# Expert weights in pairs and by layer: a new order of loading in a Mixture-of-Experts stage on one Trainium2 core

## Chip, cores and metric

One core of one Trainium2 chip. The metric is the device time of one execution in microseconds (us); given is the median of the runs. The program is written in a tile language: a pool hands out buffers, and the framework puts in the waits between engines.

## What is computed

The input x has shape (4, 128, 64, 64). Layer 0 is group normalisation, three 1x1 convolutions and a full softmax attention over 4096 positions. Layer 1 treats the positions as tokens of 128 channels: first a cumulative attention with eight heads, then a feed-forward block in which each of 64 experts chooses 8 tokens of each batch entry. Only this last block matters here:

```python
pooled = jnp.einsum('bked,bke->bed', gathered, topv)       # 4 x 64 x 128
h = jnp.concatenate([pooled.transpose(1, 0, 2), ones], axis=-1)
h = jax.nn.gelu(jnp.einsum('ebd,edh->ebh', h, weight1), approximate=False)
h = jnp.concatenate([h, ones], axis=-1)
out = jnp.einsum('ebh,eho->ebo', h, weight2)               # 64 experts, 128 -> 512 -> 128
outputs = outputs.at[jnp.arange(Bn)[:, None], flat_idx].add(weighted)
```

Each expert sees one pooled row for each of the 4 batch entries, so its two matrices (128 x 512 and 512 x 128, 256 KB each in float32) are used for 4 rows only. The 64 experts have 32 MB of weights together, and all of them are read.

## The kernel before

The layers run one after the other; the expert block comes last, its first matmul at 2313.5 us of 2414.9. Its weights lie in DRAM as `fw`, one row block for each expert: 128 partitions x (512 numbers of the first layer + 512 of the second), 512 KB in one transfer. They are kept in NW = 21 buffers: 19 from the pool `fw`, and the two resident tensors `wks` and `wvs`, which held projections of the attention before (L1135 to L1140). The 21 first loads are given out ahead of the block (L1142). All of these loads stand on SP's queue, in the order in which the source gives them out, apart from `wks` and `wvs`, whose loads stand first. A load waits on SP for the buffer's last reader, and for the eighth load before it.

The experts go in 16 groups of QG = 4. The four experts of a group lie in four strips of 32 rows of one PSUM tile, so that their matmuls run side by side. The order of PE is written out by hand (`manual_schedule`, L1176). The steps for a group g are:

- `first(g)` (L1248): four matmuls 4 x 512 into `ph`; ScalarE copies them to `hr`.
- `turn(g)` (L1261): four transposes of `hr` (`htr`), VectorE adds the bias (`hs`), ScalarE applies GELU.
- `second(g)` (L1276): sixteen matmuls into `po`, the chunk c outside, the expert u inside; VectorE copies `po` to `og`. At its end, L1287 gives out the loads of the four experts that take over the group's buffers.
- `gather(g)` (L1291): a transpose of `og` and a copy into `eot`.
- `back(n)` (L1157), as filler between: turns four blocks of the residual `t` back into channel order (`otr`) and copies them.

In the loop (L1305), groups 0 to 4 (g < AHEAD = 5) run turn(g), first(g+1), back, gather(g-1), second(g); from group 5 on it is back, turn(g), back, gather(g-1), second(g), first(g+1). Three groups before the end the fillers stop. Also in the loop, ScalarE counts chosen tokens (L1320).

After the last group the result is transposed (L1334), and for the two pairs p of batch entries 16 tiles each are made by matmul (`sct`, L1357), added to `t` by VectorE (L1364) and written out from SP's and ScalarE's queues (L1367). At the very end a test value `inside` is made (L1373, L1374); every engine loads it into a register (L1380) and branches on it (L1381). With these inputs the branch's fallback is not taken.

Of the kernel before, what the change touches and what calls it, by code (L numbers as in the profile page):

```python
# [18 lines left out]
def conv_attn_hybrid_kernel(  # L19
# [55 lines left out]
    all_ones = const.tile([P, P], F32, tag="all_ones", name="all_ones")  # L75
# [26 lines left out]
    wks = resid.tile([C, NH, C], F32, tag="wks", name="wks")  # L102
    wvs = resid.tile([C, HD], F32, tag="wvs", name="wvs")
# [210 lines left out]
    with ExitStack() as l0:  # L314
# [261 lines left out]
        first, chain, blocks = preparation(0)  # L576
# [9 lines left out]
        for n, (b, qb, p) in enumerate(steps):  # L586
# [11 lines left out]
            if (qb, p) == (q0, 0) and b + 1 < B:  # L598
                first, chain, blocks = preparation(b + 1)
# [43 lines left out]
    inside = resid.tile([P, 1], mybir.dt.int32, tag="inside", name="inside")  # L643
    within = resid.tile([P, 1], F32, tag="within", name="within")
# [19 lines left out]
    QG = 4  # L664
    QW = P // QG
# [4 lines left out]
    EG = E // QG  # L670
    NB = B * NBLK
    NW = 21

    def layer1(pre, ready):
# [6 lines left out]
        with ExitStack() as kept, ExitStack() as l1:  # L681
# [447 lines left out]
            expert_weights = {}  # L1129

            def load_expert(e):
                if e >= E:
                    return

                if e % NW >= NW - 2:  # L1135
                    w = wvs if e % NW == NW - 1 else wks.rearrange("d h e -> d (h e)")
                else:
                    w = fwp.tile([P, FH + FC * C], F32, tag="fw", name=f"{pre}fw_{e}")
                nc.sync.dma_start(out=w, in_=fw[e])
                expert_weights[e] = (w[:, :FH], w[:, FH:].rearrange("p (c o) -> p c o", c=FC))  # L1140

            for e in range(NW):  # L1142
                load_expert(e)

            eos = fo.tile([P, B // 2, C], F32, tag="eo", name=f"{pre}eo")

# [6 lines left out]
            pooled = fo.tile([C, E, B], F32, tag="pooled", name=f"{pre}pooled")  # L1153
# [18 lines left out]
            def backs(m, engine):  # L1172
                for _ in range(m):
                    back(turns.pop(0), engine)

            with tc.manual_schedule(engines={mybir.EngineType.PE}):  # L1176
# [71 lines left out]
                def first(g):  # L1248

                    ph = phs[g % 2]  # L1250
                    for u in range(QG):
                        e = g * QG + u
                        nc.tensor.matmul(
                            ph[u * QW : u * QW + B, :], pooled[:, e, :], expert_weights[e][0],
                            start=True, stop=True,
                        )
                    hr = fs.tile([P, FH], F32, tag="hr", name=f"{pre}hr_{g}")
                    nc.scalar.copy(hr, ph)
                    return hr

                def turn(g, hr):  # L1261

                    ptr = ps_a.tile([P, FC, QG, QW], F32, tag="kv", name=f"{pre}htr_{g}")
                    for c in range(FC):
                        nc.tensor.transpose(
                            ptr[:, c].rearrange("p u b -> p (u b)"), hr[:, bass.ts(c, P)], ident
                        )
                    hs = fs.tile([P, FC, QG, B], F32, tag="hs", name=f"{pre}hs_{g}")
                    nc.vector.tensor_tensor(
                        hs, ptr[:, :, :, :B],  # L1270
                        fb1s[:, bass.ts(g, QG), :].rearrange("p u c -> p c u")
                        .unsqueeze(3).to_broadcast([P, FC, QG, B]), ALU.add,
                    )
                    return hs, nc.scalar.activation(hs, hs, AF.Gelu).ins

                def second(g, hs):  # L1276
                    po = pos[:, g % 2, :]
                    for c in range(FC):
                        for u in range(QG):
                            nc.tensor.matmul(  # L1280
                                po[u * QW : u * QW + B, :], hs[:, c, u, :],
                                expert_weights[g * QG + u][1][:, c, :],
                                start=(c == 0), stop=(c == FC - 1),
                            )
                    og = fs.tile([P, C], F32, tag="og", name=f"{pre}og_{g}")
                    nc.vector.tensor_copy(og, po)
                    for u in range(QG):  # L1287
                        load_expert(g * QG + u + NW)
                    return og

                def gather(g, og):  # L1291
# [10 lines left out]
                hr = first(0)  # L1302
                og = None
                AHEAD = NW // QG
                for g in range(EG):  # L1305
                    last = g + 3 >= EG
                    if turns and g >= AHEAD and not last:
                        backs(1, nc.vector)
                    hs, gelu = turn(g, hr)
                    if g < AHEAD:  # L1310
                        hr = first(g + 1)
                    if turns and not last:
                        backs(1, nc.vector)
                    if og is not None:
                        gather(g - 1, og)
                    if ready:
                        p, k = g // NBLK, g % NBLK
                        ones_of = ps_a.tile([P, BLK], F32, tag="kv", name=f"{pre}chosen_{g}")
                        with tc.issue_after(gelu):
                            nc.scalar.activation(  # L1320
                                ones_of, lgs[p][:, bass.ts(k, BLK)], AF.Sign,
                                accum_out=count[:, p, k : k + 1],
                            )
                    og = second(g, hs)
                    if AHEAD <= g < EG - 1:
                        hr = first(g + 1)
                    if turns and g in (AHEAD, AHEAD + 1):
                        with tc.issue_after(gelu):
                            backs(1, nc.scalar)
                assert not turns  # L1330
                gather(EG - 1, og)
                for p in range(B // 2):
# [3 lines left out]
                        out=eos[:, p, :], in0=ptr, scalar=rden[:, p : p + 1], in1=eos[:, p, :],  # L1336
                        op0=ALU.mult, op1=ALU.add,
                    )
                if ready:
                    chosen = fs.tile([P, 4], F32, tag="chosen", name=f"{pre}chosen", bufs=1)  # L1340
# [3 lines left out]
                        out=chosen[:, 3:4], in0=chosen[:, 2:3], scalar1=8.5, scalar2=None, op0=ALU.is_le  # L1344
                    )

                for p in range(B // 2):

                    for k0, OB in ((0, 1), (1, 1), (2, 2), (4, 2), (6, 1), (7, 1)):
                        for k in range(k0, k0 + OB):  # L1350
                            pss = [
                                ps_a.tile([P, BLK], F32, tag="kv", name=f"{pre}sct_{p}_{k}_{z}")
                                for z in range(2)
                            ]
                            for z in range(2):
                                half = slice(z * E, (z + 1) * E)
                                nc.tensor.matmul(  # L1357
                                    pss[z], eos[half, p, :], lgs[p][half, bass.ts(k, BLK)],
                                    start=True, stop=True,
                                )  # L1360
                            for z in range(2):
                                n = (2 * p + z) * NBLK + k
                                at = t[:, bass.ts(n, CPB), :].rearrange("c i x -> c (i x)")
                                nc.vector.tensor_add(at, at, pss[z])  # L1364
# [13 lines left out]

    layer1("", True)
    inside_r = nc.values_load(inside[0:1, 0:1], min_val=0, max_val=1)  # L1380
# [59 lines left out]
```

## Time and profile before

| | us |
|---|---|
| median of 3 runs | 2416.25 (2414.59 to 2419.01) |
| the profiled execution | 2416.65 |
| its span in the trace | 2414.9 |
| matmuls of the expert block, from the first to the last | 2313.5 to 2382.0 |
| first and last load of `fw` issued | 2278.8 and 2368.0 |
| output additions (L1364), 32 | 2385.3 to 2404.5 |

The engines: PE is TensorE's matmuls and PEld its weight loads, DVE is VectorE, ACT ScalarE, POOL GpSimd, SP SyncE, which issues most of the DMAs; "SPq" is its queue. Times in the trace are counted from the start of the span. Of the whole span PE is busy for 97%, nearly all of it in the two attentions; the mean DMA rate over the span is 46 GB/s, while in the last two of 40 equal slices it is 358 and 286 GB/s. PE's clock was granted at 0.994 of full speed on average. Each matmul of the source shows as two in the trace. A matmul's end in the trace is modelled, and a few matmul records can be missing.

### The profile page before, as it was taken

The page shows a single profiled execution, that of the slowest core. Times are in us where ns is not written, and L with a number is a line of the kernel's source. Part 1 is how long each engine was busy: PE and PEld are TensorE (multiplying, and loading weights), DVE is VectorE, ACT ScalarE, POOL GpSimd, SP SyncE. Part 2 cuts the span into 40 slices and gives each one's busy share as a digit, 9 for nine tenths or more (in the row PEclk, how much of TensorE's full clock was granted, in tenths as well). Part 3 has the DMA queues.
Part 4 walks back from the last instruction along what each step waited for, and adds up shares of the span by engine and source line. Part 5 has one row for each costly group of instructions (what it writes and reads, how often), then busy time and mean ns, then how long its engine had stood idle before and what let it go on. Part 6 is the DMA issues. An engine that isn't in the chain of part 4 may idle for free.

```text
span 2414.9 us, 45766 instructions
## 1 busy us (share of the span) xinstructions
PE 2347.5 (97%) x19496; PEld 1566.0 (65%) x19496; DVE 1505.8 (62%) x2610; ACT 1208.4 (50%) x1638; POOL 304.1 (13%) x337
## 2 busy tenths in 40 slices
PE   6999999999999999999999998999999999999887
PEld 3567777677778677778777774555555555555553
DVE  5666666666655666655555555666666676776654
ACT  4444444444443444444433434666666666666541
POOL 0000000000000000000000001334333433333200
PEclk9999999999999999999999999999999999999999
DMA  2200120000100000020000000211112121112397
GB/s 76 80 22 7 29 62 1 12 18 22 49 24 1 16 13 22 18 51 1 1 1 1 1 1 19 53 39 44 48 38 54 37 55 37 38 38 54 93 358 286
DMA packets 61191, 109.95 MB, mean 46 GB/s; under 512 B 10033, under 2 KB 35121, under 8 KB 60977
## 3 DMA queue, kind: packets, MB, share of 16 engines
q1 hardware_dynamic: 57536, 101.22, 14.5%
q10 hardware_dynamic: 3440, 5.70, 0.7%
q8 instruction: 155, 2.54, 0.4%
q14 instruction: 60, 0.48, 0.1%
HBM read 85.40 MB, written 8.91 MB: 39 GB/s over the span
## 4 chain that ended last, share of the span: by engine, by line
PE 89%; DVE 5%; ACT 2%; DMA 2%; issue 1%; SPq 0%; ACTq 0%; DVEq 0%
PE av L513 36%; PE sc L488 18%; PE pk L731 9%; PE pv L849 8%; PE po L885 4%; PE pt L865 2%; PE ps L750 2%; DMA fw<-in_fw_dram 1%; PE otr L552 1%; PE po L892 1%; PE pe L430 1%; PE pa L455 1%; PE pl L942 1%; DVE t L1364 1%; PE ltr L721 1%
## 5 line engine op out<-in xcount | busy, mean ns | idle before, releaser
L513 PE MATMUL av<-pr,am 64*128 64x512 f32 x4096 | 1050.5, 591 | 0.7 <-ACT pr L492 0.7
L495 DVE TENSOR_TENSOR acc<-acc,pr 128x1024 f32<-128x1024 f32 x480 | 586.8, 1223 | 443.4 <-ACT pr L492 443.2
L492 ACT ACTIVATE pr<-sc 128x1024 f32<-128x1024 f32 x512 | 523.6, 1023 | 671.8 <-PE sc L488 603.0
L513 PEld LDWEIGHTS av<-pr,am 64*128 64x128 f32 x4096 | 636.6, 187 | 253.2 <-issue 32.3
L488 PE MATMUL sc<-e,e 64*128 64x512 f32 x2048 | 608.0, 592 | 0.0
L488 PEld LDWEIGHTS sc<-e,e 64*128 64x128 f32 x2048 | 315.2, 187 | 103.1 <-issue 14.5
L731 PE MATMUL pk<-xt,wks 128*128 128x512 f32 x512 | 244.2, 617 | 6.7 <-DVE within L660 4.2
L849 PE MATMUL pv<-wvs,xt 128*128 128x512 f32 x512 | 226.4, 595 | 2.2 <-ACT v L853 2.2
L853 ACT ACTIVATE v<-pv 128x512 f32<-128x512 f32 x256 | 152.7, 597 | 69.7 <-PE pv L849 69.6
L733 ACT ACTIVATE ks<-pk 128x512 f32<-128x512 f32 x256 | 148.5, 597 | 62.8 <-PE pk L731 62.6
L849 PEld LDWEIGHTS pv<-wvs,xt 128*128 128x128 f32 x512 | 96.9, 191 | 121.0 <-issue 113.9
L837 DVE TENSOR_TENSOR em<-em,rb 128x1024 f32<-128x1024 f32 x64 | 79.5, 1244 | 148.0 <-DMA rb<-rd 148.0
L731 PEld LDWEIGHTS pk<-xt,wks 128*128 128x128 f32 x512 | 92.1, 193 | 115.0 <-issue 82.1
L828 POOL TENSOR_TENSOR em<-et,mask 128x1024 f32<-128x1024 f32 x64 | 122.6, 1937 | 88.3 <-ACT et L815 88.3
L96 POOL TENSOR_SCALAR xg<-t,gmv,grs 128x128 f32<-128x128 f32 x120 | 95.2, 806 | 285.9 <-DVE grs L92 207.4
L885 PEld LDWEIGHTS po<-v,em 64*64 64x64 f32 x4096 | 111.6, 133 | 27.3 <-DVE before L875 26.7
L885 PE MATMUL po<-v,em 64*64 64x128 f32 x4096 | 119.6, 271 | 0.3 <-issue 0.3
L739 POOL MEMSET ew<- 128x1024 f32 x1 | 1.0, 952 | 942.1 <-PE pa L455 942.1
L787 DVE RECIPROCAL rr<-rr 128x512 f32<-128x512 f32 x32 | 107.3, 3353 | 1.1
L772 ACT ACT_TABLE_LOAD x24 | 30.8, 1283 | 119.2 <-DVE ss L771 119.2
L773 POOL COPY state<-mm 128x1 f32<-128x1 f32 x32 | 20.6, 644 | 504.7 <-DVE mm L767 504.6
L875 DVE TENSOR_TENSOR before<-before,pt 128x128 f32<-128x128 f32 x256 | 72.6, 284 | 9.6 <-PE pt L865 3.8
(189 smaller groups left out, 2075.6 us busy)
## 6 DMA issues: line engine op xcount, KB each, us to landing
rb<-rd SPq DMA_DIRECT2D x128, 256.0 KB
fw<-in_fw_dram SPq DMA_DIRECT2D x58, 512.0 KB
t<-in_xtok_dram SPq DMA_DIRECT2D x32, 256.0 KB
e<-ee SPq DMA_DIRECT2D x63, 128.0 KB
x<-in_x_dram SPq DMA_DIRECT2D x14, 512.0 KB
e<-ee SPq DMA_DIRECT2D x63, 64.0 KB
out_dram<-t SPq DMA_DIRECT2D x8, 256.0 KB
out_dram<-t ACTq DMA_DIRECT2D x8, 256.0 KB
```

Source lines behind the costliest of these rows:

```text
L96: i = engine.tensor_scalar(out=dst, in0=t[:, chunk, :], scalar1=mean, scalar2=rs, op0=ALU.subtract, op1=ALU.mult)
L488: nc.tensor.matmul(sc[:, u, :], e2[halves[u], p, :], e1[halves[u], :], start=True, stop=True)
L492: nc.scalar.activation(pr, sc, AF.Exp)
L495: added.append(nc.vector.tensor_add(acc, acc, pr).ins)
L513: nc.tensor.matmul(av, am[h, j, :], pr[h, u, :], start=(j == 0), stop=(j == NCH - 1))
L731: nc.tensor.matmul(pk, wks[:, h, :], xt, start=True, stop=True)
L733: nc.scalar.activation(ks, pk, AF.Silu)
L787: inverse = nc.vector.reciprocal(rr, rr).ins
L828: nc.gpsimd.tensor_tensor(em, eq.unsqueeze(2).to_broadcast([P, 2 * NH, H2]), mask.unsqueeze(1).to_broadcast([P, 2 * NH, H2]), ALU.mult,)
L849: nc.tensor.matmul(pv.rearrange("p h d -> p (h d)"), xt[:, bass.ts(2 * q + s, P)], wvs[:, bass.ts(m, BLK)], start=True, stop=True,)
L853: last = nc.scalar.activation(v[:, bass.ts(m, HPB), :], pv, AF.Silu).ins
L885: nc.tensor.matmul(po[s * H2 : (s + 1) * H2, u, q, :], aas[q][half, s, h, :], vs[2 * q + s][half, h, :], start=(q == 0 and h == 0), stop=F ...
```

## The change

The weights are stored in DRAM by layer and pair: `fw[layer, pair]` has 128 partitions x (two experts x 512 numbers), again 512 KB for one transfer. The 64 transfers ("units") are given out in the order of use: layer 0 of group 0; then for each group g from 1 on, layer 0 of g and layer 1 of g-1; last, layer 1 of group 15. Each of `first` and `second` gives out two units, which take over buffers in the same ring of 21. The branches on AHEAD are gone: in every group, turn(g) comes first and first(g+1) follows ahead of second(g); the back-turn of groups 5 to 12 that stood ahead of turn(g) stands behind it. In the last group, second runs its first pair of experts through all four chunks, then the second pair. The test value `inside` is made between the two pairs of batch entries instead of after them.

```diff
+            units = []
+            for g in range(EG):
+                units += [(0, 2 * g), (0, 2 * g + 1)]
+                if g:
+                    units += [(1, 2 * g - 2), (1, 2 * g - 1)]
+            units += [(1, 2 * EG - 2), (1, 2 * EG - 1)]
+            unit_weights = {}
+
+            def load_units(m):
+                for _ in range(m):
+                    n = len(unit_weights)
+                    if n >= len(units):
+                        return
+
+                    if n % NW >= NW - 2:
+                        w = wvs if n % NW == NW - 1 else wks.rearrange("d h e -> d (h e)")
+                    else:
+                        w = fwp.tile([P, FH + FC * C], F32, tag="fw", name=f"{pre}fw_{n}")
+                    nc.sync.dma_start(out=w, in_=fw[units[n][0], units[n][1]])
+                    unit_weights[units[n]] = w
+
+            def layer_weights(layer, e):
+                w = unit_weights[layer, e // 2].rearrange("p (i x) -> p i x", i=2)[:, e % 2, :]
+                return w.rearrange("p (c o) -> p c o", c=FC) if layer else w
+
+            load_units(NW)
...
                         nc.tensor.matmul(
-                            ph[u * QW : u * QW + B, :], pooled[:, e, :], expert_weights[e][0],
+                            ph[u * QW : u * QW + B, :], pooled[:, e, :], layer_weights(0, e),
                             start=True, stop=True,
                         )
+                    load_units(2)
                     hr = fs.tile([P, FH], F32, tag="hr", name=f"{pre}hr_{g}")
...
-                    for c in range(FC):
-                        for u in range(QG):
-                            nc.tensor.matmul(
-                                po[u * QW : u * QW + B, :], hs[:, c, u, :],
-                                expert_weights[g * QG + u][1][:, c, :],
-                                start=(c == 0), stop=(c == FC - 1),
-                            )
+                    m = QG // 2 if g + 1 == EG else QG
+                    for u0 in range(0, QG, m):
+                        for c in range(FC):
+                            for u in range(u0, u0 + m):
+                                nc.tensor.matmul(
+                                    po[u * QW : u * QW + B, :], hs[:, c, u, :],
+                                    layer_weights(1, g * QG + u)[:, c, :],
+                                    start=(c == 0), stop=(c == FC - 1),
+                                )
                     og = fs.tile([P, C], F32, tag="og", name=f"{pre}og_{g}")
                     nc.vector.tensor_copy(og, po)
-                    for u in range(QG):
-                        load_expert(g * QG + u + NW)
+                    load_units(2)
                     return og
...
                     last = g + 3 >= EG
+                    hs, gelu = turn(g, hr)
                     if turns and g >= AHEAD and not last:
                         backs(1, nc.vector)
-                    hs, gelu = turn(g, hr)
-                    if g < AHEAD:
+                    if g + 1 < EG:
                         hr = first(g + 1)
...
                     og = second(g, hs)
-                    if AHEAD <= g < EG - 1:
-                        hr = first(g + 1)
...
                 for p in range(B // 2):
+                    if ready and p:
+                        good = ps_a.tile([P, BLK], F32, tag="kv", name=f"{pre}good")
+                        nc.tensor.matmul(good[:, 0:1], all_ones, chosen[:, 3:4], start=True, stop=True)
+                        nc.vector.tensor_scalar(
+                            out=inside, in0=good[:, 0:1], scalar1=float(P), scalar2=within,
+                            op0=ALU.is_ge, op1=ALU.mult,
+                        )
...
-                if ready:
-                    good = ps_a.tile([P, BLK], F32, tag="kv", name=f"{pre}good")
-                    nc.tensor.matmul(good[:, 0:1], all_ones, chosen[:, 3:4], start=True, stop=True)
-                    nc.vector.tensor_scalar(
-                        out=inside, in0=good[:, 0:1], scalar1=float(P), scalar2=within,
-                        op0=ALU.is_ge, op1=ALU.mult,
-                    )
```

More of the change, by code (lines that the diff above doesn't have):

```diff
@@ L1127, in layer1 @@
             ps_p = pool("l2p", space=PSUM)
[L1129 to L1143, printed above, removed]
+            units = []
[20 more added lines that the diff above has]
+            load_units(NW)
             eos = fo.tile([P, B // 2, C], F32, tag="eo", name=f"{pre}eo")
@@ L1414 @@
         "gb": a["L1_ffn_gate_b"].reshape(-1, 1),
-        "fw": np.concatenate(
+        "fw": np.stack(
             [
@@ L1418 @@
                 fw2[:, :FH, :].reshape(E, FH // 128, 128, D).transpose(0, 2, 1, 3).reshape(E, 128, -1),
-            ],
-            axis=2,
-        ),
+            ]
+        ).reshape(2, E // 2, 2, 128, -1).transpose(0, 1, 3, 2, 4).reshape(2, E // 2, 128, -1),
         "fb1": fw1[:, D, :].reshape(E, FH // 128, 128).transpose(2, 0, 1),
```

## The prediction, made before the changed kernel had run

> **What bounds the kernel now.** I first read the slices of the page: PE is at nine tenths until the last twentieth of the span, and only there do the DMA engines fill (9 and 7 tenths; 358 and 286 GB/s in the last two slices). The change touches only that stretch, so the rest is taken as unchanged. Next I read the chain of waits in order of time (start, length, what), for the end of the expert layers:
>
> ```profile
> 2345.68 1.06 PE po L1280 x32
> 2346.73 0.83 PE ph L1253 x4
> 2347.57 10.15 DMA fw<-in_fw_dram
> 2357.77 10.17 DMA fw<-in_fw_dram
> 2368.01 10.11 DMA fw<-in_fw_dram
> 2378.16 1.03 PE ph L1253 x2
> 2379.27 0.59 ACT hr L1258
> 2379.91 0.66 PE htr L1265 x4
> 2380.57 0.12 PE ogtr L1294
> 2380.69 0.22 DVE hs L1269
> 2380.93 0.27 ACT hs L1274
> 2381.24 1.15 PE po L1280 x32
> ...
> 2385.31 19.20 DVE t L1364 x32
> ```
>
> From 2347.6 to 2378.2 nothing but weight transfers is on the chain: the last expert's weights arrive at 2378.16, and only then do its first layer, copy, turn, GELU and second layer run, one after the other, until 2382.39. That is a tail of 4.23 us behind the last byte. Then come the output additions. Why do the weights end so late? I asked for the DMA share by stretches of 2 us (busy times of PE, PEld, DVE, ACT, POOL; then clock, DMA share, GB/s) and for what the SP queue waited on between 2298 and 2320 (total, times, longest):
>
> ```profile
> 2312.00:2314.00 2.00, 0.75 (x9) 0.28 (x9) 0.89 (x4) 0.00 (x0) 0.00 (x0) 1.00 0.51 199
> 2314.00:2316.00 2.00, 1.18 (x12) 0.42 (x4) 0.00 (x0) 0.59 (x1) 0.00 (x0) 1.00 0.02 6
> 2316.00:2318.00 2.00, 2.00 (x30) 0.96 (x33) 0.56 (x2) 1.46 (x4) 0.00 (x0) 1.00 0.00 0
> 2318.00:2320.00 2.00, 2.00 (x36) 0.85 (x24) 0.88 (x3) 0.50 (x2) 0.00 (x0) 1.00 0.26 43
> ```
>
> ```profile
> SPq L1139 <- PE po L1280: 12.8, 1, 12.8
> ```
>
> ```profile
> 2318.63 0.33 SPq L1139 DMA_DIRECT2D fw<-in_fw_dram  x1
> ```
>
> The first 21 loads fill all buffers; the 22nd waits 12.8 us for the first group's second layer (po, 2317.56 to 2318.62) and is issued at 2318.63. The engines stand idle from about 2313 to 2319.5. From 2324 until 2374 their share is 0.99 to 1.06 at about 405 GB/s: SP issues a 512 KB load every 1.28 us (2362.89, 2364.17, 2365.46, ...). So the end of the weights is: the restart (2318.63) plus 43 loads. 43 x 1.28 = 55.0 us; the measured stretch to 2378.16 is 59.5, so 4.5 us are start, slow beginning (344 GB/s from 2320 to 2324) and completion.
>
> Last, one step of PE while weights are plentiful, from the same chain:
>
> ```profile
> 2321.86 0.59 PE htr L1265 x4
> 2322.44 0.97 PE ph L1253 x8
> 2323.41 0.59 PE otr L1162 x4
> 2324.00 0.11 PE ogtr L1294
> 2324.11 0.99 PE po L1280 x32
> ```
>
> A group of four experts costs PE 3.25 us with one output block turned back (otr), but 4 x 1.28 = 5.1 us of DMA. PE outruns the loads, as its waits for weights (7.2 us, 7 times) confirm.
>
> [...] I use the measured 1.28 us for 512 KB. [...] here 32 matmuls of 273 ns take 1.06 us in all, because four experts lie in four strips. [...] here it took 1118 ns (SP, L1380), which I use.
>
> **The change, part by part.**
>
> *Loads by layer and pair.* The same 64 transfers of 512 KB, rows of 4 KB each. The order of instructions shows the same queue on SP with the same 8 in flight, so I take 1.28 us for each as before. In the before, a buffer is free after its expert's second layer; in the after, buffers 0 and 1 are free after the first layer of group 0. PE ran that from 2313.55 for 1.04 us, until 2314.59, against 2318.62: the restart comes 4.03 us earlier, into engines shown idle. Does the flow then tear? Two loads at 2314.6 last until about 2318.3; first(1) ends at 2317.04 and frees two, second(0) at 2318.62 two more. Afterwards PE frees four per 3.25 us and DMA needs 5.1. The first microseconds are thinner than before (two in flight, then four), which the trace does not show: between 0 and 0.5 us lost. I take 0.1: gain 3.9 us, last weights at T = 2374.3.
>
> *PE order.* From group 5 on, first(g+1) now stands between turn(g) and second(g), and the back-turn ahead of turn(g) comes after it. Nothing is added; it needs cover only if PE becomes late. PE from 2331.6 (five steps of 3.25 after 2315.4): groups 5 and 6 with three back-turns 2.66 + 3 x 0.59 = 4.43 each, 7 to 12 with two 3.84 each, 13 and 14 with none 2.66: group 15's first layer would be wanted at 2331.6 + 8.9 + 23.0 + 2.7 + 0.6 = 2366.8. Its weights land four loads ahead of the last, T - 5.1 = 2369.2. DMA remains the later by 2.4 us: cost nothing. GELU's chain (htr to po start 1.33 us: 0.76, 0.26, 0.31 in the timeline at 2374.86) lies behind first(g+1) and the back-turns.
>
> *The tail.* The last unit is now only the second layer of experts 62 and 63. Second(14) waits for the load two before the last, T - 2.56; it occupies PE for 0.99, so turn(15) starts at T - 1.6 and po at T - 0.27. Pair by pair, two strips instead of four run side by side. Matmuls of one strip follow each other at 0.107 us (starts 2355.72, 2355.83, 2355.94), eight of them per pair: 0.86 us for each pair, whatever the other strips do. The first pair issues until T + 0.6, the second until T + 1.45, and the last matmul ends 0.17 later: T + 1.6. Bounds: if a pair takes half of 1.06, T + 0.8; if both take 1.06 in full, T + 1.9. Against 4.23 the gain is 2.6 (2.3 to 3.4). The three small DVE steps on counts (chosen, until GELU + 1.45 = T + 0.9) stay ahead of og, hidden behind po.
>
> *The test in the middle.* `inside` (good, two matmuls; DVE 0.21 us) moves between the two halves of the additions: +0.2 us on DVE's chain, while its place at the end was not ahead of ScalarE's last output DMA. So +0.2 (0 to 0.4). SP now loads the register there: 1.12 + 0.25 us in which its next output issue waits, some 0.8 us late. Hidden: output transfers fill the DMA engines from 2391 to 2409 (share 0.98 to 1.06), some 4 us behind issue. Without that backlog it would cost up to 0.8.
>
> Sum: -3.9 - 2.6 + 0.2 = -6.3 us. The profiled execution took 2416.65 us (span 2414.9): 2410.35. The median shown is 0.4 lower, so 2410.0.
>
> **The rivals.**
> (a) *The early restart is lost*, because the wait for a buffer is not released by first(0), or because PE becomes the last to be ready. For: only 2.4 us of slack against PE, some 0.2 us per step. Against: the loads' waits are on PE alone, and each step is made of shown durations. Then -2.6 + 0.2 = -2.4: 2413.8.
> (b) *More than forecast*: the first pair hides wholly, and a continuous flow avoids the slow beginning (344 instead of 405 GB/s over 4 us is 0.6 us): -4.0 - 3.4 - 0.6 = -8.0, 2408.3.
> (c) *Slower*: putting first(g+1) ahead of second(g) makes PE, in order, stand at first(g+1) for weights while second(g) could run and free buffers; steps then wait for DMA and DMA for steps. It decides once the eight steps of groups 5 to 12 exceed 5.3 us instead of about 4 (2331.6 + 8 x 5.3 + 8.5 = 2382.5, the old end of po); at 6 us it ends 5.6 us later: 2421.9. Against: loads of those groups are issued 10 us and more before they are wanted.
>
> **How the numbers follow.** About 0.2% (4.8 us) is what a measurement can tell from no change. Forecast 0.75, (a) 0.13, (b) 0.08, (c) 0.04. Bounds of the forecast: -3.5 - 2.3 + 0.4 = -5.4 to -4.0 - 3.4 = -7.4, thus 2410.9 to 2408.9; the three runs shown spread over 4.4 us, so 1.5 to 2 us more on each side: 2407.3 to 2412.9, which takes in (b) and leaves (a) and (c), 0.17, out. Faster by over 0.2%: forecast and (b), less some 0.04 for the spread, 0.79; same 0.17; slower 0.04.
>
> **What would show it.** Right: the 22nd load is issued near 2314.6 and SP's long wait names ph; T near 2374.3; po ends 1.6 us after the last weights; first output addition near 2378.8. Wrong: a restart at 2318.6, a DMA share under 0.95 between 2320 and 2370, or PE waiting for GELU instead of weights in groups 13 to 15.

## The result and the profile after

| | before | changed | |
|---|---|---|---|
| median, 8 runs each on one chip, us | 2417.15 (2414.59 to 2421.43) | 2407.59 (2405.75 to 2412.43) | ratio 0.9961, 95% interval 0.995 to 0.9971: 7 to 12 us less |
| the profiled execution, us | 2416.65 | 2405.75 | 10.90 less |
| its span, us | 2414.9 | 2404.0 | 10.9 less |

Forecast were 2410.0 us and a fall of 6.3. The changed kernel measured once more, on another chip, gave 2407.73 (5 runs) beside 2416.55 for the kernel before (9 runs), ratio 0.9964 (0.995 to 0.9978).

The change begins to act at first(0), the first matmul of the expert stage. That one starts at 2313.55 in the profile before and at 2310.11 in the profile after. Over all the profiles of this study, whose program ahead of it is the same but for the order of the first loads (and e11's added transposes), it starts anywhere from 2310.1 to 2313.6. So 3.44 of the 10.90 us lie in work that the change does not touch, and two single profiles must not be compared by their ends. All stage times below therefore count from the start of first(0). The table gives when each stage is over, and in its fourth column by how much the stage itself became longer or shorter; "landed" is the last completion of a transfer in the trace.

| us from the start of first(0) | before | changed | difference of the stage | forecast for it |
|---|---|---|---|---|
| 22nd load issued | 5.08 | 1.07 | -4.01 | -4.03 |
| last weights landed (T) | 64.57 | 61.39 | +0.83 behind the restart, -3.18 with it | +0.1, -3.9 with it |
| last group's second layer (po) done | 68.75 | 62.73 | -2.84 | -2.6 |
| first output addition starts | 71.74 | 65.66 | -0.06 | 0 |
| last output addition ends | 90.96 | 85.15 | +0.27 | +0.2 |
| end of the span | 101.37 | 93.90 | -1.66 | 0 |
| sum | | | -7.47 | -6.3 |

Three readings of the changed kernel's trace answer to the lines shown of before. First, what SP's queue waits for between 2290 and 2380 (total, times, longest):

```profile
SPq L1149 <- DMA fw<-in_fw_dram: 33.6, 35, 1.9
...
SPq L1149 <- PE ph L1266: 13.0, 5, 8.4
SPq L1149 <- PE po L1296: 3.8, 7, 1.0
```

The long wait is now for ph, the first layer, as forecast; the wait for po is cut to pieces of at most 1.0 us. Second, the restart itself in the timeline, and the same stretch in steps of 2 us (the last three columns are TensorE's granted clock, the DMA engines' share and GB/s):

```profile
2310.11 1.04 PE L1266 MATMUL ph<-fw,pooled 128*4 128x512 f32 x8 [0.43 <-DVE pooled L1201]
2311.18 4.49 SPq L1149 DMA_DIRECT2D fw<-in_fw_dram  x4
...
2311.93 1.09 PE L1279 MATMUL htr<-ident,hr 128*128 128x128 f32 x4 [0.77 <-ACT hr L1272]
2312.95 1.89 PE L1266 MATMUL ph<-fw,pooled 128*4 128x512 f32 x8
```

```profile
2310.00:2312.00 2.00, 1.11 (x9) 0.21 (x10) 0.01 (x1) 0.58 (x1) 0.00 (x0) 1.00 0.10 35
2312.00:2314.00 2.00, 2.00 (x12) 0.73 (x12) 0.22 (x1) 0.68 (x2) 0.00 (x0) 0.50 0.93 260
2314.00:2316.00 2.00, 2.00 (x24) 1.05 (x24) 0.25 (x1) 0.77 (x3) 0.00 (x0) 0.65 0.84 283
2316.00:2318.00 2.00, 2.00 (x40) 0.94 (x28) 0.96 (x3) 0.42 (x2) 0.00 (x0) 1.00 0.87 307
2318.00:2320.00 2.00, 2.00 (x42) 1.41 (x39) 0.77 (x2) 0.94 (x3) 0.00 (x0) 1.00 1.04 391
```

The 22nd load leaves SP 0.03 us after first(0) ends, and the DMA engines work where they stood idle before. But from 2312.0 to 2315.4 TensorE ran at half its clock: the second first layer took 1.89 us instead of 1.04, so the next buffers came back late and the flow stayed thin (260 to 307 GB/s) until 2318. The kernel before had no such stretch in the expert stage's start in its profile (clock 1.00 in every 2 us from 2310 to 2320, its second first layer 1.04 us). The experiments below put the 0.83 of the table down to it. Third, the tail:

```profile
2371.05 0.26 ACT L1288 ACTIVATE hs<-hs 128x64 f32<-128x64 f32 x1 [2.81 <-DVE hs L1283]
...
2371.35 0.72 PE L1296 MATMUL po<-wvs,hs 128*4 128x128 f32 x10 [0.53 <-ACT hs L1288]
...
2372.13 0.71 PE L1296 MATMUL po<-fw,hs 128*4 128x128 f32 x10
...
2372.90 0.29 DVE L1302 COPY og<-po 128x128 f32<-128x128 f32 x1 [0.40 <-PE po L1296]
```

The last weights landed at 2310.11 + 61.39 = 2371.50. po starts 0.15 us ahead of that and ends 1.35 after it, against 4.18 before. The stretch from 2320 to 2360 moved 399 to 408 GB/s at a DMA share of 1.02 or more: the loads still set the pace.

### The profile page after: what moved, and what is told of

It is laid out like the page before. It is cut to its first block, busy times and chain, and to the rows that moved or that the text cites. A ratio compares the mean times of both kernels' runs of the same rounds, so it can differ in the third digit from the quotient of the medians.

```text
span 2404.0 us, 45784 instructions
## 1 busy us (share of the span) xinstructions
PE 2342.3 (97%) x19496; PEld 1563.9 (65%) x19496; DVE 1504.9 (63%) x2610; ACT 1207.8 (50%) x1638; POOL 303.4 (13%) x337
## 4 chain that ended last, share of the span: by engine, by line
## 5 line engine op out<-in xcount | busy, mean ns | idle before, releaser
L733 ACT ACTIVATE ks<-pk 128x512 f32<-128x512 f32 x256 | 148.4, 597 | 60.1 <-PE pk L731 59.8
```

Of the source, the lines that this page charges most:

```text
L733: nc.scalar.activation(ks, pk, AF.Silu)
```

## The experiments

Each kernel ran 5 to 21 times beside the kernel before; "changed" is the kernel of the change. The table puts all of them beside each other; the columns from "half clock" on are taken from each one's trace, one profile for each kernel. "Half clock" says whether TensorE's granted clock was halved for 3.4 us at first(0).

| kernel | median us | ratio to before (95%) | half clock | 22nd load | T | T less 22nd | T to po's end | last addition to end |
|---|---|---|---|---|---|---|---|---|
| before | 2417.15 | | no | 5.08 | 64.57 | 59.49 | 4.18 | 10.41 |
| changed | 2407.59 | 0.9961 (0.995, 0.9971) | yes | 1.07 | 61.39 | 60.32 | 1.35 | 8.75 |
| changed, again | 2407.73 | 0.9964 (0.995, 0.9978) | yes | 1.07 | 62.01 | 60.94 | 1.38 | 8.54 |
| e1 test last | 2410.34 | 0.9973 (0.9963, 0.9983) | yes | 1.07 | 61.87 | 60.80 | 1.37 | 10.42 |
| e2 restart late (text) | 2407.54 | 0.9961 (0.9947, 0.9974) | yes | 1.07 | 61.52 | 60.45 | 1.35 | 8.67 |
| e3 four wide | 2407.29 | 0.9961 (0.9947, 0.9974) | no | 1.07 | 60.23 | 59.17 | 1.09 | 8.81 |
| e4 before, test in the middle | 2414.44 | 0.9991 (0.9984, 0.9997) | no | 5.08 | 64.19 | 59.12 | 4.18 | 8.78 |
| e5 second layer first | 2406.51 | 0.9962 (0.9949, 0.9976) | no | 1.07 | 60.87 | 59.80 | 1.10 | 8.71 |
| e6 first layer last | 2412.41 | 0.9983 (0.9975, 0.9991) | yes | 1.07 | 61.75 | 60.68 | 7.15 | 8.68 |
| e7 no branch | 2406.24 | 0.9957 (0.9944, 0.9971) | yes | 1.07 | 61.72 | 60.65 | 1.39 | 6.88 |
| e8 two ahead | 2407.31 | 0.9958 (0.9945, 0.9972) | no | 1.07 | 60.53 | 59.47 | 1.09 | 8.63 |
| e9 buffers held | 2410.68 | 0.9977 (0.9967, 0.9986) | yes | 5.74 | 64.82 | 59.08 | 1.34 | 8.69 |
| e10 first layer last, TensorE busy | 2410.27 | 0.9974 (0.9966, 0.9981) | no | 1.07 | 60.42 | 59.35 | 4.63 | 8.78 |
| e11 busy start | 2406.80 | 0.9963 (0.995, 0.9977) | no | 1.07 | 60.57 | 59.50 | 1.09 | 8.72 |

The interval of a median is some 2 to 3 us wide on each side, so the single terms are read from the columns of the traces; the medians say only whether the direction holds. Where nothing acts on them, the 22nd load, T to po's end and the last addition to the end repeat within 0.3 us, T less the 22nd within 0.7 us among profiles of the same clock.

**e1, the test at its old place.**

```diff
-                    if ready and p:
-                        good = ...
+                if ready:
+                    good = ...
```

(the block moved from between the halves to behind the last addition)

> The changed kernel with the test for `inside` put back behind the last output addition; the loads stay as changed. Theory of the forecast (the test's old place cost nothing at the end): 0.2 us faster than the changed kernel, so about 9.4 us faster than before, and 8.8 us from the last addition to the end of the span. Theory formed on the result (the test, the five register loads and the fetch of the instructions behind the branch come after the last output is queued, and end later than it): 1.5 us slower than the changed kernel, about 8.1 us faster than before, and 10.2 to 10.5 us from the last addition to the end of the span.

Measured: 10.42 us from the last addition to the end, as in the kernel before (10.41), against 8.75 and 8.54 in the changed kernel; 2.7 us slower than the changed kernel by the medians. The forecast's theory falls: the test's place was worth 1.7 to 1.9 us behind the last addition, less the 0.28 by which the additions were shorter here.

**e2, the first layer's buffers given back later in the text.**

```diff
-                    load_units(2)
                     hr = fs.tile([P, FH], F32, tag="hr", name=f"{pre}hr_{g}")
...
-                    load_units(2)
+                    load_units(4)
                     return og
```

> The changed kernel with the first layer's buffers given back where the second layer's are: first() issues no loads, second() issues four. Theory of the forecast (the early restart of the loads is worth 4.0 us): the 22nd load is issued 5.1 us after first(0) begins instead of 1.1, and the kernel is 3.5 to 4.0 us slower than the changed one. Rival (the early restart is lost in the flow, all of the gain being at the tail): no slower than the changed kernel by more than 0.5 us.

Measured: nothing changed (2407.54), and the two theories are not told apart: the 22nd load was still issued at 1.07. SP's longest wait was still for ph (8.8 us), the last reader of the load's buffer, though the load was asked for later in the program. Moving the request was no undoing of the change.

**e3, the last group four experts wide.**

```diff
-                    m = QG // 2 if g + 1 == EG else QG
+                    m = QG
```

> The changed kernel with the last group's second layer four experts wide, as in the other groups. In the profile of the changed kernel the first pair begins only 0.15 us before the last weights land, so the pair by pair order hides little: theory of the result, within 0.4 us of the changed kernel on either side, with po's end 1.1 to 1.4 us after the last weights. Rival (the pair by pair order carries the shorter tail): 0.7 to 1.0 us slower, po's end 2.0 to 2.4 us after the last weights.

Measured: 2407.29, no difference by the medians; po ends 1.09 us after the last weights, 0.26 sooner than in the changed kernel. T is not the right mark for this, though. Counted from the landing of the load two before the last, on which second(14) waits, po ends 3.84 us later in each of the seven profiles with pairs (changed twice, e1, e2, e5, e7, e9) and 3.56 to 3.58 later in the three that are four wide (e3, e8, e11). The pair by pair order costs 0.27 us here; the rival falls. (e5 has 1.10 behind T with pairs because its last load landed 2.74 instead of 2.50 us after that one.)

**e4, the kernel before with the test in the middle alone.**

```diff
                 for p in range(B // 2):
+                    if ready and p:
+                        good = ...
...
-                if ready:
-                    good = ...
```

> The kernel before with only the test for `inside` moved between the two halves of the outputs; loads as before. Theory of the forecast: 0.2 us slower than before. Theory formed on the result: the last addition ends 0.2 to 0.3 us later and the end of the program comes 1.6 us sooner after it, so 1.2 to 1.5 us faster than before.

Measured: 1.9 us faster than before by the medians (0.7 to 3.9), 8.78 instead of 10.41 from the last addition to the end; the additions took 0.28 longer. By the trace -1.63 + 0.28 = -1.35, the number expected. Two programs, one edit, in both directions: the place of the test is worth 1.4 us, and it is independent of the loads.

**e5, another order meant to delay the restart.**

```diff
             units += [(1, 2 * EG - 2), (1, 2 * EG - 1)]
+            units = units[4:6] + units[:4] + units[6:]
```

> The changed kernel with the first group's second layer put at the head of the loads, so that the 22nd load, which takes the first buffer again, waits for the end of second(0) as in the kernel before (giving the buffers back later in the program text, as an earlier run did, left the order of the loads as it was and delayed nothing). Theory (the early restart carries three to four us): the 22nd load is issued 5.1 us after first(0) begins instead of 1.1, the last weights land 64.2 to 64.6 us after it instead of 60.2 to 61.5, and the time is 3.0 to 4.0 us above the changed kernel's, about 5.5 to 6.5 us below before. Rival (the restart is lost again in the flow, since the next loads wait for second(0) in either kernel): less than 1 us above the changed kernel.

Measured: 2406.51, the 22nd load again at 1.07, and SP's longest wait still for ph. The edit did not delay the restart either, so it says nothing on its worth; why the 22nd load did not have to wait for second(0) is not shown. As a second run of nearly the changed kernel, without the half clock, it is useful: T came at 60.87.

**e6, the last group's first layer loaded last.**

```diff
+            units = units[:-6] + units[-4:] + units[-6:-4]
...
-                    if g + 1 < EG:
+                    if g + 2 < EG:
                         hr = first(g + 1)
...
                     og = second(g, hs)
+                    if g + 2 == EG:
+                        hr = first(g + 1)
```

> The changed kernel with the last group's first layer loaded last and its first(15) put after second(14): the two layers of the last group stand behind the last weights again, as before. Theory (the shorter tail is the layer order's): from the last weights to po's end 4.0 to 4.4 us instead of 1.1 to 1.4, the time 2.5 to 3.1 us above the changed kernel's. Rival (something else bounds the end of the loop): less than 1 us above.

Measured: 4.8 us slower than the changed kernel by the medians, and 7.15 us from the last weights to po's end: the direction of the theory, with nearly twice the size. The trace says why. The windows over the tail (TensorE's granted clock is the third number from the end):

```profile
2370.00:2372.00 2.00, 0.42 (x12) 0.12 (x4) 0.29 (x1) 0.00 (x0) 0.00 (x0) 1.00 1.01 395
2372.00:2374.00 2.00, 0.81 (x3) 0.10 (x4) 0.00 (x0) 0.00 (x0) 0.00 (x0) 0.56 0.32 129
2374.00:2376.00 2.00, 2.00 (x8) 0.10 (x4) 0.00 (x0) 0.00 (x0) 0.00 (x0) 0.50 0.00 0
2376.00:2378.00 2.00, 1.26 (x7) 0.93 (x5) 0.00 (x0) 0.58 (x1) 0.00 (x0) 0.50 0.00 0
2378.00:2380.00 2.00, 1.54 (x18) 0.81 (x20) 0.80 (x5) 0.87 (x3) 0.00 (x0) 0.50 0.00 0
```

and the matmul after the wait, for four experts' first halves:

```profile
2373.18 1.87 PE L1267 MATMUL ph<-wvs,pooled 128*4 128x512 f32 x4 [2.76 <-DMA wvs<-in_fw_dram]
```

TensorE stood 2.76 us for weights; 1.83 us into this wait its clock fell to half, and it stayed so through the whole tail. The edit had changed two things at once.

**e9, the buffers really held.** Both edits of order having failed, this one adds a reader: eight matmuls of one column, whose results the next matmuls overwrite.

```diff
                     m = QG // 2 if g + 1 == EG else QG
+                    for e in range(2 * QG if g == 0 else 0):
+                        nc.tensor.matmul(
+                            po[e % QG * QW : e % QG * QW + B, 0:1], pooled[:, e, :],
+                            layer_weights(0, e)[:, 0:1], start=True, stop=True,
+                        )
```

> The changed kernel with eight one-column matmuls more at the head of second(0), which read the first layer's weights of groups 0 and 1 and whose results the next matmuls overwrite: these eight buffers can't come back before second(0), so that the restart of the loads is late as in the kernel before, which two edits of the load order didn't bring about. Theory (the early restart carries three to four us): the 22nd load is issued 5.0 to 5.5 us after first(0) begins instead of 1.1, the last weights land 63.8 to 64.8 us after it instead of 60.2 to 61.9, and the time is 2.5 to 4.0 us above the changed kernel's. Rival (the flow after an early restart is so thin that a late one in a burst catches up): the last weights at most 62.5 us after first(0), less than 1 us above.

Measured: the restart came at 5.74, SP's long wait names the added matmuls (line 1294):

```profile
SPq L1149 <- PE po L1294: 13.0, 1, 13.0
```

T came at 64.82, 3.43 after the changed kernel's 61.39 (2.81 after its other profile), and the medians are 3.1 us apart. So a restart 4.67 us later puts the last weights 2.8 to 3.4 us later, in profiles in which TensorE was at half clock at first(0) in both. (The edit holds the loads 0.66 us longer than the kernel before does, so the early restart of the change carries somewhat less than this at half clock.) The rival, that the flow eats the restart, falls.

**e10, e6 without TensorE's wait.** As e6, with twelve transposes of a block of tokens that nobody reads ahead of first(15).

```diff
                     if g + 2 == EG:
+                        for n in range(3):
+                            fill = ps_a.tile([P, CPB, P], F32, tag="kv", name=f"{pre}fill_{n}")
+                            for c in range(CPB):
+                                nc.tensor.transpose(fill[:, c, :], t[:, c, :], ident)
                         hr = first(g + 1)
```

> As the run with the last group's first layer loaded last, with twelve transposes of a block of tokens, read by nobody, between second(14) and first(15), so that TensorE doesn't stand 2.8 us before the last weights. Theory (that run's 7.2 us behind the last weights were 4.2 of work and 3 of TensorE's clock at half speed after its wait): full clock from the last weights on, 4.0 to 4.4 us from them to po's end, and the time 2.5 to 3.1 us above the changed kernel's. Rival (the half clock has another cause): 6.5 us or more to po's end and 4 us or more above.

Measured: the clock is whole in every window of the tail, and the same four matmuls wait 1.30 us and take 1.03 instead of 1.87:

```profile
2368.49 1.53 PE L1345 MATMUL fill<-ident,t 128*128 128x128 f32 x12
2371.32 1.03 PE L1267 MATMUL ph<-wvs,pooled 128*4 128x512 f32 x4 [1.30 <-DMA wvs<-in_fw_dram]
```

4.63 us from T to po's end, 3.3 more than in the changed kernel, and 2.7 us slower by the medians: with both layers of the last group behind the last weights the tail of the kernel before is back. (It is 0.45 above 4.18; two pairs in turn take 1.52 where four experts abreast take 1.06.) The order by layer carries the short tail, and the rival on the half clock falls too in these profiles, one of each kernel: adding useless work to TensorE made e6 2.1 us faster by the medians (the intervals overlap).

**e7, no branch.**

```diff
-    inside_r = nc.values_load(inside[0:1, 0:1], min_val=0, max_val=1)
-    with tc.If(inside_r == 0):
-        load_projections()
-        shifted_layer0()
-        layer1("g_", False)
```

> The changed kernel without the register load of `inside`, the branch and the recomputation behind it (left out: the recomputation for inputs whose scores are out of range, which these inputs don't need). Theory (with the test early, the end hangs on the landing of the last output, no longer on SyncE's register load and branch): 8.0 to 8.7 us from the last addition to the end of the span instead of 8.8, 0.1 to 0.8 us below the changed kernel. Rival (register loads and branches still stand in the end's way): more than 1.5 us below the changed kernel.

Measured: 6.88 us from the last addition to the end, 1.9 less than in the changed kernel's first profile and 1.7 less than in its second, so the theory I had formed on the result was wrong in this point: by the traces the rival's bound of 1.5 is passed (the medians are 1.4 and 1.5 us apart). With the test early the register load is out of the way, but the branch is not. SP's instructions at the end, in us after the end of the last addition (the page does not list register loads and branches; these are from the trace):

| | before | e1 | changed | e7 |
|---|---|---|---|---|
| SP loads the register | 0.16 to 1.28 | 0.16 to 1.29 | -9.69 to -8.67 | - |
| SP branches | 1.67 | 1.69 | -0.05 | - |
| SP's next instruction | 7.30 | 7.26 | 5.72 | -0.03 |
| last output landed | 7.22 | 6.22 | 6.68 | 5.81 |
| SP through with its waits for outputs | 8.52 | 8.46 | 7.6 | 6.1 |
| GpSimd starts to clear the semaphores | 9.98 | 9.99 | 8.32 | 6.49 |
| end | 10.41 | 10.42 | 8.75 | 6.88 |

Behind the branch SP has no instruction for 5.5 to 5.8 us; in that time the traces have DMA packets of instructions (8 or 16 KB each), in the midst of the last outputs' packets. From the last addition on there are 12 such packets in before and e1, 10 in the changed kernel, and one in e7, which has no branch. The branch itself took 0.05 us on SP, in before and in the changed kernel; the 5.5 to 5.8 us lie behind it. That SP waits in the gap for the instructions behind the branch is my reading of these packets, not shown. In e1 the last output had landed 1 us before SP got its next instruction: there SP, not the outputs, set the end. That answers for 0.9 us of the 1.66; the other 0.7 is GpSimd, which took 1.16 us from the start of its last drain to the clearing before, and 0.42 after. In the changed kernel it had branched long before (-8.56, its next instruction at -4.53). That the 0.7 is a wait for instructions too is argued, not shown: it was not tried by itself.

**e8, the first layer two groups ahead.**

```diff
-                hr = first(0)
+                hrs = [first(0), first(1)]
...
-                    hs, gelu = turn(g, hr)
+                    hs, gelu = turn(g, hrs[g])
...
-                    if g + 1 < EG:
-                        hr = first(g + 1)
+                    if g + 2 < EG:
+                        hrs.append(first(g + 2))
```

(units in the same order as used, and the last group four experts wide)

> The changed kernel with the first layer run two groups ahead (first(0) and first(1) back to back, then first(g+2) after turn(g)), the loads in that order, and the last group's second layer four experts wide. Theory (after the early restart the flow is still thin until second(0) gives its buffers back): loads 24 and 25 are issued 2.1 us after first(0) begins instead of 3.9 to 4.8, the last weights land 0.4 to 1.2 us sooner after it, po ends 1.1 us after them, and the time is 0.5 to 1.4 us below the changed kernel's. Rival (TensorE becomes the bound): no gain or a loss, with TensorE never waiting for weights in the last groups.

Measured: 2407.31, no gain over the changed kernel. Loads 24 and 25 were issued at 1.96 and 2.44 instead of 4.75 and 5.17, but the 22nd landed at 5.51 instead of 4.63, and T less the restart is 59.47, in the middle of what the kernels without half clock have (e3, four wide too, has 59.17). Neither theory holds: the weights arrived no sooner with more loads under way at the start, and TensorE, which still waited for weights three times (1.8 us), didn't become the bound.

**e11, TensorE kept busy around first(0).** As e3, with ten transposes that nobody reads in TensorE's three waits there.

```diff
+                    if p:
+                        fill(CPB, "a")
...
+                fill(2, "b")
                 hr = first(0)
+                fill(CPB, "c")
```

> The changed kernel with the last group's second layer four experts wide, and with ten transposes of a block of tokens that nobody reads in TensorE's three waits around first(0) (four, two and four). In the profiles so far TensorE's clock was halved for 3.4 us at first(0) in some and not in others; where it was, and the loads restarted early, the last weights landed 60.3 to 60.8 us after the 22nd load's issue, elsewhere 59.1 to 59.8. Theory (a busy TensorE doesn't get the half clock there, as one run showed at the end of the loop): full clock from first(0) on, the last weights 59.1 to 59.8 us after the 22nd load, first(0) at most 0.3 us later, and the time 0 to 1.0 us below the changed kernel's. Rival (the half clock comes from something else): it is there in spite of the transposes, or the transposes cost more than it.

Measured: the clock stayed whole and T less the restart is 59.50:

```profile
2312.00:2314.00 2.00, 1.81 (x16) 0.95 (x16) 0.11 (x1) 0.59 (x1) 0.00 (x0) 1.00 0.31 59
2314.00:2316.00 2.00, 2.00 (x37) 1.07 (x33) 0.67 (x2) 1.41 (x4) 0.00 (x0) 1.00 0.97 371
```

2406.80 against 2407.73 of the changed kernel measured beside it: the right side, but within the noise. One profile with a whole clock would prove little where others without transposes had it too. But in all the traces the clock changes only on a grid of 3.41 us (last section), and here a step of it fell 1.42 us after first(0) began: in all seven profiles without the transposes in which it fell between 1.26 and 1.88, the clock was halved. That speaks for the theory, by one profile.

**The changed kernel once more.**

> The changed kernel itself, on the chip of the run beside it. Both theories: its earlier time within its interval, 8 to 10 us below before; from the 22nd load's issue to the last weights 60.3 to 60.8 us if TensorE's clock is halved at first(0), 59.1 to 59.8 if not.

Measured: 8.8 us below before; half clock, and 60.94 from the restart to T. In this profile the chain that ended last can be followed back through the tail (start, us, what):

```profile
2361.66 10.16 DMA wks<-in_fw_dram
...
2371.86 1.04 PE po L1296 x28
2372.91 0.60 PE htr L1279 x4
...
2373.60 0.23 DVE hs L1283
...
2373.86 0.27 ACT hs L1288
...
2374.17 1.52 PE po L1296 x32
...
2375.71 0.30 DVE og L1302
```

The last weights landed at 2312.27 + 62.01 = 2374.28, 0.11 after the last po had begun. The chain doesn't pass through them: it comes from the load two before, landed at 2371.82, through second(14), turn(15) and po to po's end, 3.84 us in all.

## Why the forecast was right, and where not

**The restart: right; its size only where TensorE keeps its clock.** The forecast had the 22nd load issued 4.03 us sooner and lost 0.1 in a thinner flow. It came 4.01 sooner. Five profiles with the early restart and a whole clock at first(0) (e3, e5, e8, e10, e11) have T at 60.2 to 60.9, mean 60.52; the two with the late restart and a whole clock (before, e4) 64.57 and 64.19, mean 64.38: 3.86 apart, where 3.9 was forecast. The first step that failed is "Does the flow then tear?": it bounded the loss by 0.5 us, with TensorE's steps as long as in the profile before. In the six profiles with half clock and early restart T less the restart is 60.3 to 60.9, against 59.2 to 59.8 without: 1.2 us more on the mean (60.64, 59.46), since there the second pair of buffers comes back late (load 24 issued at 4.75 to 4.78 instead of 3.47 in e3, e5, e10 and e11). The late restart of e9 had the half clock too and lost nothing (59.08); it gave its first buffers back in one burst (seven loads issued in the 3.21 us from 2317.10), which I take for the reason; that was not tried by itself.

**The tail: right.** Forecast 1.6 after T with po starting at T - 0.27; measured 1.35 and T - 0.15, a gain of 2.84 for the forecast 2.6. The start was 0.1 later than forecast, and po took 1.5 us for the forecast 1.9, since the two pairs overlap: in the trace the second pair's matmuls begin at 2371.80, while the first pair's go on until 2372.4. e10 shows that it is the order by layer. What the diff names, pair by pair, is not what brings it: po starts when turn(15) is through, 0.1 to 0.15 us ahead of the last weights (0.39 in e5), so the first pair cannot use the 1.3 us that its weights are there sooner, and the strips then run mostly two at a time (1.52 us of po instead of 1.06). turn(15) stands behind second(14) on TensorE; whether putting it ahead would let the pairs pay was not tried.

**The test in the middle: the second step that failed.** The forecast took -0 for the end, because "its place at the end was not ahead of ScalarE's last output DMA". That looked at what the test delays, an output, and not at what stands behind the test: five engines' register loads and branches, and SP's waits for all outputs behind its branch. The price of the register load was even in the forecast (1.12 + 0.25 us, "hidden" where it goes) but not credited where it comes from. The other half was sized right: +0.27 on the additions for +0.2. Net -1.4 instead of +0.2.

**TensorE's order: right.** Nothing shows that first(g+1) ahead of second(g) cost anything. TensorE's weight loads waited for weights 4.2 us in 6 waits between 2310 and 2380, instead of 7.2 us in 7 waits before. Some 3 us of that lie up to first(15), so TensorE stayed ahead of the loads, as forecast (2.4 us of slack).

**The rivals.** (a), the early restart lost, and (c), TensorE late, did not happen. (b), more than forecast, has the size of what was measured but not its reasons: the first pair is not hidden, and the beginning is slower, not faster.

**The sum.** With the end priced as measured, the forecast's terms give -3.9 - 2.6 + 0.2 - 1.65 = -7.95; the trace from first(0) on gives -7.47 in the first profile and 94.35 - 101.37 = -7.02 in the second, both with half clock, and -8.83 in e3 without. The medians' 8.8 and 9.6 lie somewhat above and their intervals (5 to 12, 7 to 12) take them in. How often TensorE loses its clock at first(0) in executions that are not profiled stays open, and so does the rest of some 2 us between these two profiles and the medians. The forecast range, 2407.3 to 2412.9, holds the measured 2407.59 by 0.3 us, and that is in part luck: the terms alone gave 2408.9 to 2410.9, the range was widened for the spread of the runs, and the loss to the half clock offset part of the gain at the end that the forecast had left out.

No version tried beats the changed kernel by more than the noise; e5, e11, e3, e8 and e7 (which leaves the recomputation out) lie 0.3 to 1.4 us lower.

## What to carry to other kernels

In this kernel the ring of buffers restarted when SP's wait for the last reader of a buffer ended: with both layers of an expert in one buffer, 5.08 us after first(0) began, at the end of second(0); with each buffer given to one step of the work and the loads ordered by use, at 1.07, at the end of first(0). Where a ring waits like this, that split brings the restart with the first step rather than the last. To undo such a change for a test, add a reader (e9: 5.74); moving the request in the text moved nothing here (e2: 1.07). Computing earlier what the branch at the end tests brought 1.4 us (e4): price the program's end by the instruction that the last queue reaches last (in e1 SP's first behind its branch, at 7.26), not by the last output (there landed at 6.22).

## What was not expected of the hardware

- TensorE's clock fell to half for 3.41 us or a multiple of it (10.24 us in e6's tail). In each of the 14 traces every change of it stands on one grid of 3.41 us: in the changed kernel at 2264.21, 2267.62, 2311.99, 2315.41 and 2397.33, which are 1, 13, 1 and 24 steps apart. Where the grid lies against the program differs from one profile to the next, and this tells the profiles apart at first(0):

  | profile | a step of the grid, us after first(0) begins | TensorE busy in the 3.41 us before it | clock behind it |
  |---|---|---|---|
  | before, e3, e4, e5, e8, e10 | 0.73 to 0.95 | 1.86 | whole |
  | e7, e2, changed again | 1.26 to 1.36 | 1.55 to 1.65 | half |
  | e6, e1, e9, changed | 1.59 to 1.88 | 1.34 to 1.41 | half |
  | e11, with transposes | 1.42 | 2.67 | whole |

  TensorE has waits of 1.12, 0.43 and 0.77 us here; the last one begins when first(0) is through, 1.04 us after its start, so a later step has more of it in the 3.41 us before. In e6's tail the step fell 1.83 us into the wait, TensorE busy for 1.30 of the 3.41 us before; in e10 it fell 0.24 us before the end of the wait, with 2.35 us busy, 1.53 of them the transposes.

  No wait in these stretches lasted the 3.41 us of a step (the longest was 2.76), and yet the clock was halved behind 1.30 to 1.65 us of work in a step and whole behind 1.86 to 2.67. That the busy share of the step before decides is my reading of these profiles, not shown, and no share that keeps the clock is: elsewhere in the changed kernel's trace the clock stayed whole behind a step that was busy for 0.43 of its time (up to 2288.10) and was halved behind one of 0.60 (up to 1458.66).
- Work that nobody reads paid here: 1.53 us of transposes ahead of a wait took 2.5 us off e6's tail (e10: 7.15 to 4.63), in one profile of each.
- Behind a branch at the end of the program, with the last outputs under way, SP's next instruction came 5.5 to 5.8 us later; leaving the register load and the branch out brought the end 1.7 to 1.9 us forward (e7).
- After the stop, the first load of the restart landed 3.4 to 3.9 us after its issue, 4.45 in e8 with four issued together. The stream of 43 loads took 59.1 to 59.5 us from a late restart in a burst (before, e4, and e9 at half clock), and from an early one in pairs 59.2 to 59.8 us where TensorE had its clock, 60.3 to 60.9 where not.
